# A graph layer on one core: six edges in a partition instead of eight, a written order with the MLP in pieces, and the check of dst at the end

## The chip, the cores and the metric

The kernel runs on one core of a Trainium2 chip. The metric is the device time of one launch in microseconds, taken as the median over runs.

## The reference

One layer of a graph network over 12,500 nodes and 412,500 edges, in fp32. `dst` (the second row of `edge_index`) is sorted.

```
h   = maximum(layernorm(x), 0)                        # x: 12500 x 128
agg = segment_sum(edge_attr_48, dst, 12500)           # edge_attr_48: 412500 x 48
z   = concatenate([h, agg, u], axis=1)                # u: 64 numbers, the same for every node
out = x + relu(z @ W1 + b1) @ W2 + b2                 # W1: 240 x 256, W2: 256 x 128
```

## The kernel before

**Edges.** The sum over edges is done as matmuls. A chunk is 1,024 consecutive edges, T = 8 in each of 128 partitions; a group is CG = 4 chunks, 4,096 edges, and there are 101 groups. Because `dst` is sorted, the edges of a chunk fall into a window of W = 48 consecutive nodes. VectorE compares each edge's node number, relative to its window's start (`rel`), with 0 to 47 (L194): that makes a one-hot tile `oh` of 32 x 48 columns per group. TensorE then multiplies, for each of the 32 sets of 128 edges, the edge attributes (weights, 128 x 48) with the one-hot (moving, 128 x 48) into one PSUM bank (L201). Even sets go to PSUM partitions 0 to 47, odd ones to 64 to 111, that is to the two halves of the array's columns. An fp32 matmul appears in the trace as two weight loads and two matmul instructions, so a group has 64 of each. VectorE adds the bank into `aggT` at a node that it reads from a register (`add`, L214). Edge tiles have 8 buffers and are loaded on SyncE's queue (L174).

**Nodes.** A block is 512 nodes (25 blocks, the first has 212). For each, `mlp` (L382 to L414) normalizes x on ScalarE (L390), transposes it on TensorE (L392), copies it to `hT` (L395), and for each half `a` of the hidden layer multiplies `hT` (L399) and `aggT` (L400) with weights of 128 columns, applies relu on ScalarE (L402), multiplies with `w2` (L407), adds `xb` (x + b2, made on GpSimd at L386) and stores. `normalize` (L364 to L380) does the statistics of up to four blocks at once: 16 pairs of L372 and L373.

**Order.** The program is written as groups 0 to 5, then the check of `dst`, then groups 6 to 100 with a whole `mlp` between groups when a block's edges are done. The framework's planner moves instructions by its own cost estimates: in the trace, 20 matmuls of L201 stand between the second and the third matmul instruction of L407. The check (L267 to L280) tests that all edges fall into their windows; a branch (L284) behind it holds a slow general pass. For these inputs all do, and the branch is not taken.

**Names used below.** `dst` becomes `rel` by `read_dst` (four pieces, with transposes at L237 and copies at L238). `load_x` (L353) loads x for up to four blocks into one of two buffers.

## Time and profile before

| what | us |
|---|---|
| median of 3 runs | 422.22 |
| lowest and highest | 418.25, 425.51 |
| the profiled execution | 418.65 |
| its span, first to last instruction | 416.9 |
| mean granted TensorE clock | 0.957 of full speed |
| DMA traffic | 95.20 MB |

The profile is of one execution. PE is the matmul part of TensorE and PEld its weight loads, which overlap. DVE is VectorE, ACT ScalarE, POOL GpSimd, SP SyncE. A matmul's recorded duration holds its latency; the pace is read from the starts of successive instructions. "[0.43 <-ACT hT L395]" behind a row means 0.43 us of idle time on that engine, ended by that instruction.

### The profile page before, as it was taken

The numbers are of one execution on the slowest core, as the hardware profiler recorded it, in microseconds if no ns is written. First come the engines' busy times: TensorE is split into PE (matmuls) and PEld (weight loads), VectorE is DVE, ScalarE is ACT, GpSimd is POOL, SyncE is SP. The second block draws the span as 40 slices with busy tenths as digits, with TensorE's granted clock in tenths as the row PEclk, the third lists the DMA queues.
The fourth block names the chain that finished last, engine by engine and source line by source line (L and its number), as shares of the span: only waits on it lengthen the run. The fifth ranks groups of instructions, "written<-read, shape, count | busy, mean of one in ns | idle before, by whom it ended". The sixth has DMA issues, their size and how long they took to land.

```text
span 416.9 us, 15948 instructions
## 1 busy us (share of the span) xinstructions
PE 342.9 (82%) x7193; PEld 270.0 (65%) x7194; DVE 283.7 (68%) x472; ACT 106.4 (26%) x193; POOL 81.0 (19%) x41
## 2 busy tenths in 40 slices
PE   0487569998699989898986997995979998888985
PEld 0377555785477677577565777774768776757853
DVE  7898598764965696786377788467675668629510
ACT  1140027312213303331230330330321332131231
POOL 9300021120221120222022022112022112203200
PEclk9995689999999999999899999999889999989999
DMA  5997693559847978877596697696583898654000
GB/s 163 323 370 264 207 346 126 188 197 308 286 141 239 323 255 304 281 248 233 179 322 217 225 316 233 192 342 219 198 302 109 257 325 270 194 198 156 29 13 39
DMA packets 61720, 95.20 MB, mean 228 GB/s; under 512 B 2760, under 2 KB 54996, under 8 KB 61649
## 3 DMA queue, kind: packets, MB, share of 16 engines
q1 hardware_dynamic: 57287, 87.26, 62.4%
q10 hardware_dynamic: 4362, 6.89, 4.7%
q8 instruction: 57, 0.93, 0.9%
q14 instruction: 14, 0.11, 0.1%
HBM read 87.74 MB, written 6.40 MB: 226 GB/s over the span
## 4 chain that ended last, share of the span: by engine, by line
PE 40%; issue 17%; DMA 10%; DVE 10%; POOL 5%; ACT 3%; DVEq 1%; ACTq 0%; POOLq 0%
PE ps L201 17%; DMA xt<-in_x_dram 10%; PE po L407 8%; PE ph L399 7%; PE ph L400 6%; POOL xb L386 5%; DVE oh L194 4%; DVE st L372 3%; ACT hT L395 3%; PE pt L392 2%; DVE mv L373 1%; DVE ot L409 1%; DVE aggT L214 1%; DVEq L207 1%; ACT hid L402 0%
## 5 line engine op out<-in xcount | busy, mean ns | idle before, releaser
L201 PE MATMUL ps<-oh,e 128*48 128x48 f32 x6448 | 175.8, 214 | 39.4 <-issue 17.7
L201 PEld LDWEIGHTS ps<-oh,e 128*48 128x48 f32 x6448 | 163.2, 130 | 53.8 <-DVE oh L194 21.9
L194 DVE TENSOR_TENSOR oh<-iota,rel 128x1536 f32<-128x1536 f32 (+1 forms) x101 | 194.0, 1936 | 2.3 <-ACT rel L238 1.3
L386 POOL TENSOR_TENSOR xb<-xt,b_sb 128x512 f32<-128x512 f32 (+1 forms) x25 | 67.7, 2709 | 313.6 <-DVE ot L409 273.6
L395 ACT COPY hT<-pt 128x512 f32<-128x512 f32 (+1 forms) x25 | 26.9, 1076 | 186.3 <-PE pt L392 186.3
L399 PE MATMUL ph<-hT,w1h 128*128 128x512 f32 (+1 forms) x100 | 56.4, 647 | 8.0 <-ACT hT L395 7.9
L214 DVE TENSOR_TENSOR aggT<-aggT,ps 112x141 f32 (+1 forms) x101 | 29.6, 293 | 47.8 <-PE ph L400 44.0
L407 PEld LDWEIGHTS po<-w,hid 128*128 128x128 f32 (+1 forms) x400 | 49.9, 189 | 16.5 <-issue 10.4
L407 PE MATMUL po<-w,hid 128*128 128x128 f32 (+1 forms) x400 | 55.4, 281 | 1.2 <-ACT hid L402 1.1
L409 DVE TENSOR_TENSOR ot<-po,xb 128x512 f32<-128x512 f32 (+1 forms) x25 | 17.2, 688 | 51.3 <-PE po L407 49.0
L400 PE MATMUL ph<-aggT,w1a 112*128 112x512 f32 (+1 forms) x100 | 52.0, 602 | 0.0
L402 ACT ACTIVATE hid<-ph,bias 128x512 f32<-128x512 f32 (+1 forms) x50 | 33.6, 676 | 47.5 <-PE ph L400 47.5
L390 ACT ACTIVATE xn<-xt,sh,sc 128x128 f32<-128x128 f32 (+1 forms) x100 | 40.7, 484 | 3.7 <-DVE sh L378 3.7
L372 DVE BATCH_NORM_STATS2 st<-xt 128x6 f32<-128x128 f32 (+1 forms) x100 | 25.1, 262 | 22.0 <-DMA xt<-in_x_dram 22.0
L400 PEld LDWEIGHTS ph<-aggT,w1a 112*128 112x128 f32 x100 | 20.3, 203 | 24.6 <-issue 24.0
L399 PEld LDWEIGHTS ph<-hT,w1h 128*128 128x128 f32 x100 | 18.3, 204 | 23.0 <-ACT hT L395 10.3
L392 PE MATMUL pt<-ident,xn 128*128 128x128 f32 (+1 forms) x100 | 18.1, 296 | 1.6 <-ACT xn L390 1.2
L373 DVE BATCH_NORM_AGGREGATE mv<-st 128x2 f32<-128x6 f32 (+1 forms) x100 | 15.6, 162 | 0.0
L246 PE MATMUL pb<-one,brow 1*128 1x1 f32 (+1 forms) x8 | 2.0, 312 | 14.6 <-DVE brow L141 13.8
L392 PEld LDWEIGHTS pt<-ident,xn 128*128 128x128 f32 (+1 forms) x100 | 11.1, 144 | 3.8 <-POOL xb L386 1.3
L376 ACT ACTIVATE sc<-mv,eps 128x16 f32<-128x16 f32 (+1 forms) x7 | 2.1, 305 | 42.0 <-DVE mv L373 42.0
L238 ACT COPY rel<-ptd 128x512 f32<-128x512 f32 (+1 forms) x8 | 6.7, 910 | 20.7 <-DMA w1a<-in_L_gnn_W_dram 13.4
(46 smaller groups left out, 59.9 us busy)
## 6 DMA issues: line engine op xcount, KB each, us to landing
e<-in_edge_attr_dram SPq DMA_DIRECT2D x100, 768.0 KB, 7.5
xt<-in_x_dram ACTq DMA_DIRECT2D x6, 1024.0 KB
out_dram<-ot SPq DMA_DIRECT2D x24, 256.0 KB, 5.3
di<-in_dst_dram SPq DMA_DIRECT2D x3, 512.0 KB, 11.1
e<-in_edge_attr_dram SPq DMA_DIRECT2D x1, 384.0 KB, 6.5
e<-in_edge_attr_dram SPq DMA_DIRECT2D x1, 159.0 KB
w1h<-in_L_gnn_W_dram ACTq DMA_DIRECT2D x1, 128.0 KB
w<-in_L_gnn_W_dram ACTq DMA_DIRECT2D x1, 128.0 KB, 4.2
```

The costliest lines, as they stand in the source:

```text
L194: nc.vector.tensor_tensor(oh[:, :n * T], iota[:, None, :W].to_broadcast([P, n * T, W]), r[:, :, None].to_broadcast([P, n * T, W]), OP.is_e ...
L201: nc.tensor.matmul(ps[h:h + DE, STEP * k:STEP * k + W], e[:, k, t * DE:(t + 1) * DE], oh[:, k * T + t, :], start=(k == 0 and t < 2), stop= ...
L214: nc.vector.tensor_tensor(aggT[:K2, ds(at, wg)], aggT[:K2, ds(at, wg)], ps[:K2, :wg], OP.add)
L372: nc.vector.bn_stats(st[:m, i * R + r, :], xs[j][:m, r, :])
L386: nc.gpsimd.tensor_tensor(xb[:m], xs[j][:m], b2_sb[:m, None, :].to_broadcast([m, R, D]), OP.add)
L390: nc.scalar.activation(xn[:m, r], xs[j][:m, r], AF.Relu, bias=shift[j][:m, r:r + 1], scale=scale[j][:m, r:r + 1])
L392: nc.tensor.transpose(pt[:, r, :m], xn[:m, r], ident[:m, :m])
L395: nc.scalar.copy(hT[:, :n].rearrange("d (p r) -> d r p", r=R), pt[:, :, :m])
L399: nc.tensor.matmul(ph[:, :n], w1h[:, a * P:(a + 1) * P], hT[:, :n], start=True, stop=False)
L400: nc.tensor.matmul(ph[:, :n], w1a[:K2, a * P:(a + 1) * P], aggT[:K2, SL + a0:SL + a0 + n], start=False, stop=True)
L402: nc.scalar.activation(hid[:, a, :, :m], ph[:, :n].rearrange("h (p r) -> h r p", r=R), AF.Relu, bias=bias[:, a:a + 1])
L407: nc.tensor.matmul(po[:m, r], hid[:, a, r, :m], w2[:, a], start=(a == 0), stop=(a == NH - 1))
```

## The change

- A chunk is 768 edges (T = 6), a group is 6 chunks, 4,608 edges: 90 groups. The window has W = 36 nodes and is placed from the node of the group's middle edge. A group has 36 sets of 128 edges, so 72 weight loads and 72 matmul instructions; a one-hot tile has 36 x 36 columns.
- The order is written out (`manual_schedule`). In turn g: `contract(g)` on TensorE, the one-hot of g+1, the load of group g+7 (7 edge buffers), `add(g-1)`, the store of a finished block, up to three steps of statistics, and at most two pieces of the MLP (`hidden(j, 0)`, `hidden(j, 1)`, `transpose(j+1)`, `output(j)`).
- In `hidden` and `output`, every matmul with 128 weight columns becomes two with 64 columns, to the two halves of the array's columns.
- `xb` moves from GpSimd to VectorE. L373 goes; a few operations per four blocks take its place. x has three buffers.
- At the start, the first three groups get their window numbers by a load of their own (`di0`, rows of 24 bytes, and `lo0`), `dst` is read in five pieces between groups, and `aggT` is zeroed by GpSimd and ScalarE.
- The check of `dst` is summed on ScalarE (`check_dst`), decided near the end, and the branch stands behind all stores; in it is a second pass over everything.

The core of the diff (the second pass, the bodies of the check and the constants of the start are left out):

```diff
-    T = 8
+    T = 6
     CE = P * T
-    CG = 4
+    CG = 6
     GE = CG * CE
-    STEP = N * CE // E
-    SL = 8
-    W = 48
-    WG = STEP * (CG - 1) + W
+    SL = 6
+    W = 36
+    OFF = [round(N * CE / E * (k - CG / 2)) - SL for k in range(CG)]
+    PAD = -OFF[0]
+    WG = OFF[-1] - OFF[0] + W
...
-    NB = -(-NCH // P)
+    GB = P // CG
+    CB = GB * CG
+    NB = -(-NG // GB)
+    FIRST = 3
...
+    XBUFS = 3
+    PF = 7
+    LAG = 2
+    GSTEP = N * GE / E
+    LEAST = int(-OFF[0] - SL - 64)
+    NC = N + PAD + P
...
+    supers += [rest[:1]] + [rest[i:i + XB] for i in range(1, len(rest), XB)]
+    super_of = {j: s for s, js in enumerate(supers) for j in js}
+
+
+    ready = [min(NG - 1, int(-(-(a + R * m + PAD + 1 - LEAST) // GSTEP)) - 1) for a, m in blocks]
+
+    ctx.enter_context(tc.manual_schedule())
...
+    def load_group(g):
+        if g < NG:
+            edges[g] = ep.tile([P, CG, T * DE], F32, name="e")
+            load_edges(edges[g], g * CG, chunks[g])
+
...
+        middle = dst[:FIRST * GE].rearrange("(a g e) -> a g e", a=1, e=GE)[:, :, GE // 2]
+        nc.sync.dma_start(lo0, middle.to_broadcast([P, FIRST]))
+        nc.sync.dma_start(di0, dst[:FIRST * GE].rearrange("(c p t) -> p c t", p=P, t=T))
+        load_group(0)
+        nc.sync.dma_start(first[:, :nf], dst[:nf * GE].rearrange("(a g e) -> a g e", a=1, e=GE)[:, :, GE // 2])
...
+        load_group(1)
+        dis = {0: load_dst(0)}
+        load_group(2)
...
+    cut = NC * 5 // 8
+    for c in range(0, cut, 1024):
+        nc.gpsimd.memset(aggT[:, c:min(c + 1024, cut)], 0.0)
...
+    load_x(0)
+    acc = []
+    for i in range(3):
+        ps = psum.tile([P, 512], F32, name=f"ps{i}")
+        nc.scalar.copy(ps, zero.to_broadcast([P, 512]))
+        acc.append(ps)
+    load_x(1)
+    nc.scalar.copy(aggT[:, cut:], zero.to_broadcast([P, NC - cut]))
+    warm = const.tile([P, 1], F32)
...
+    def onehot(g):
+        if g < NG:
+            n = chunks[g]
+            oh = ohp.tile([P, CG * T, W], F32, name="oh")
+            rel, c = (rel0, g * CG) if g < FIRST else (rels[g // GB], g % GB * CG)
+            r = rel[:, c:c + n, :].rearrange("p c t -> p (c t)")
+            nc.vector.tensor_tensor(oh[:, :n * T], iota[:, None, :].to_broadcast([P, n * T, W]),
+                                    r[:, :, None].to_broadcast([P, n * T, W]), OP.is_equal)
+            hots[g] = oh
+
+    def contract(g):
+        n, e, oh, ps = chunks[g], edges.pop(g), hots.pop(g), acc[g % len(acc)]
+        for k in range(n):
+            o = OFF[k] - OFF[0]
+            for t in range(T):
+                h = HI * (t % 2)
+                nc.tensor.matmul(
+                    ps[h:h + DE, o:o + W], e[:, k, t * DE:(t + 1) * DE], oh[:, k * T + t, :],
+                    start=(k == 0 and t < 2), stop=(k == n - 1 and t >= T - 2), skip_group_check=True)
+
+    def add(g):
+        wg = OFF[chunks[g] - 1] - OFF[0] + W
+        _, at = nc.values_load_multi_w_load_instructions(
+            lo_i[0:1, g:g + 1], engines=[DVE], min_val=0, max_val=N - 1,
+            skip_runtime_bounds_check_because="clamped to 0..N-1 on the chip")
+        to = aggT[:K2, ds(at[0], wg)]
+        nc.vector.tensor_tensor(to, to, acc[g % len(acc)][:K2, :wg], OP.add)
...
+    def shift_dst(b, di):
+
+        rows = rows_in[b]
+        pb = pst.tile([P, 1], F32, name="pt")
+        nc.tensor.matmul(pb[:rows], brow.rearrange("a g k -> a (g k)")[:, b * CB:b * CB + rows], one,
+                         start=True, stop=True)
+        nc.vector.tensor_copy(base[:rows, b:b + 1], pb[:rows])
+        df = dp.tile([P, CE], F32, name="df")
+        nc.vector.tensor_tensor(df[:rows], di[:rows], base[:rows, b:b + 1].to_broadcast([rows, CE]), OP.subtract)
+        return df
...
+    def spread(b, df):
+
+        rows = rows_in[b]
+        dv = df.rearrange("c (p t) -> c t p", t=T)
+        rels[b] = dp.tile([P, CB, T], F32, name="rel", bufs=2)
+        for t0 in range(0, T, 3):
+            pt = pst.tile([P, 3, P], F32, name="pt")
+            for t in range(3):
+                nc.tensor.transpose(pt[:, t, :rows], dv[:rows, t0 + t, :], ident[:rows, :rows])
+            nc.scalar.copy(rels[b][:, :rows, t0:t0 + 3].rearrange("p c t -> p t c"), pt[:, :, :rows])
+
+    def check_dst(b, df):
+
+        rows = rows_in[b]
+        for s, sign in ((0, -1.0), (1, 1.0)):
+            far = dp.tile([P, CE], F32, name="far")
+            nc.scalar.activation(far[:rows], df[:rows], AF.Relu, bias=bounds[:rows, s:s + 1], scale=sign,
+                                 accum_out=span[:rows, b, s:s + 1])
+
...
+        def variance():
+
+            me, qe, mo, qo = [st[:m, :q, i] for i in (1, 2, 4, 5)]
...
+            nc.scalar.activation(sc[:m, :q], va[:m, :q], AF.Sqrt, bias=eps[:m], scale=1.0 / D)
+
+        def finish():
+            nc.vector.reciprocal(sc[:m, :q], sc[:m, :q])
+            nc.vector.scalar_tensor_tensor(sh[:m, :q], su[:m, :q], -0.5, sc[:m, :q], OP.mult, OP.mult)
...
+                stats.append((s, lambda i=i, j=j, r=r: nc.vector.bn_stats(st[:m, i * R + r, :], xs[j][:m, r, :])))
+        stats.append((s, variance))
+        stats.append((s, finish))
...
+    def transpose(j):
+        m = blocks[j][1]
+        pt = pst.tile([P, R, P], F32, name="pt")
+        xn = xns.pop(j)
+        for r in range(R):
             nc.tensor.transpose(pt[:, r, :m], xn[:m, r], ident[:m, :m])
 
-        hT = mp.tile([P, BN], F32, name="hT")
-        nc.scalar.copy(hT[:, :n].rearrange("d (p r) -> d r p", r=R), pt[:, :, :m])
-        hid = mp.tile([P, NH, R, P], F32, name="hid")
-        for a in range(NH):
-            ph = psh.tile([P, BN], F32, name="ph")
-            nc.tensor.matmul(ph[:, :n], w1h[:, a * P:(a + 1) * P], hT[:, :n], start=True, stop=False)
-            nc.tensor.matmul(ph[:, :n], w1a[:K2, a * P:(a + 1) * P], aggT[:K2, SL + a0:SL + a0 + n],
-                             start=False, stop=True)
-            nc.scalar.activation(hid[:, a, :, :m], ph[:, :n].rearrange("h (p r) -> h r p", r=R),
-                                 AF.Relu, bias=bias[:, a:a + 1])
+        hT = mp.tile([P, P, R], F32, name="hT")
+        nc.scalar.copy(hT[:, :m], pt[:, :, :m].rearrange("d r p -> d p r"))
+        hTs[j] = hT.rearrange("d p r -> d (p r)")
+
+    def hidden(j, a):
+        a0, m = blocks[j]
+        n = R * m
+        if a == 0:
+            hids[j] = mp.tile([P, NH, R, P], F32, name="hid")
+            xb = mp.tile([P, R, D], F32, name="xb")
+            nc.vector.tensor_tensor(xb[:m], xs[j][:m], b2_sb[:m, None, :].to_broadcast([m, R, D]), OP.add)
+            xbs[j] = xb
+        ph = psh.tile([P, BN], F32, name="ph")
+        for c in (0, HI):
+            nc.tensor.matmul(ph[c:c + HI, :n], w1h[:, a * P + c:a * P + c + HI], hTs[j][:, :n],
+                             start=True, stop=False, skip_group_check=True)
+        for c in (0, HI):
+            nc.tensor.matmul(ph[c:c + HI, :n], w1a[:K2, a * P + c:a * P + c + HI], aggT[:K2, PAD + a0:PAD + a0 + n],
+                             start=False, stop=True, skip_group_check=True)
+        nc.scalar.activation(hids[j][:, a, :, :m], ph[:, :n].rearrange("h (p r) -> h r p", r=R),
+                             AF.Relu, bias=bias[:, a:a + 1])
+
+    def output(j):
+        m = blocks[j][1]
         po = pso.tile([P, R, D], F32, name="po")
         for r in range(R):
             for a in range(NH):
-                nc.tensor.matmul(po[:m, r], hid[:, a, r, :m], w2[:, a], start=(a == 0), stop=(a == NH - 1))
+                for c in range(0, m, HI):
+                    k = min(m, c + HI)
+                    nc.tensor.matmul(po[c:k, r], hids[j][:, a, r, c:k], w2[:, a], start=(a == 0), stop=(a == NH - 1),
+                                     skip_group_check=True)
+        pos[j] = po
+
+    def store(j):
+        a0, m = blocks[j]
         ot = mp.tile([P, R, D], F32, name="ot")
-        nc.vector.tensor_tensor(ot[:m], po[:m], xb[:m], OP.add)
+        nc.vector.tensor_tensor(ot[:m], pos.pop(j)[:m], xbs.pop(j)[:m], OP.add)
         k = m - m % 16
...
+    pieces = []
+    for j in range(len(blocks)):
+        at = ready[j] + LAG
+        if j == 0:
+            pieces.append((2, lambda j=j: transpose(j)))
+        pieces.append((at, lambda j=j: hidden(j, 0)))
+        pieces.append((at + 1, lambda j=j: hidden(j, 1)))
+        if j + 1 < len(blocks):
+            pieces.append((at + 2, lambda j=j: transpose(j + 1)))
+        pieces.append((at + 2, lambda j=j: output(j)))
...
+    def pop_piece():
+        nonlocal freed
+        pieces.pop(0)[1]()
+        if hTs:
+            prepare(max(hTs) + 1)
+        if freed < len(supers) and xbs and max(xbs) == supers[freed][-1]:
+            load_x(freed + XBUFS)
+            freed += 1
...
+    for g in range(NG + LAG):
+        if g < NG:
+            contract(g)
+            if g == 1:
+                spread(0, dfs[0])
+            onehot(g + 1)
+            load_group(g + PF)
+            b, i = divmod(g, GB)
+            if b + 1 < NB:
+                if i == GB - 14:
+                    dis[b + 1] = load_dst(b + 1)
+                elif i == GB - 9:
+                    dfs[b + 1] = shift_dst(b + 1, dis[b + 1])
+                elif i == GB - 7:
+                    spread(b + 1, dfs[b + 1])
+                elif i == GB - 5:
+                    check_dst(b + 1, dfs[b + 1])
+            if g == 0:
+                dfs[0] = shift_dst(0, dis[0])
+            elif g == 2:
+                first_bias()
+            elif g == 3:
+                check_dst(0, dfs[0])
+            elif g == NG - 6:
+                decide()
+        if 0 <= g - 1 < NG:
+            add(g - 1)
+        for j in late:
+            store(j)
+        for _ in range(3):
+            if stats:
+                stats.pop(0)[1]()
+        if g == 1:
+            prepare(0)
+        n = 0
+        while pieces and pieces[0][0] <= g and n < 2:
+            pop_piece()
+            n += 1
+        late = list(pos)
+    while pieces:
+        pop_piece()
...
+    isbad = nc.values_load(bad[0:1, 0:1], min_val=0, max_val=1,
+                           skip_runtime_bounds_check_because="clamped to 0..1 on the chip")
+    with tc.If(isbad >= 1):
```

## Rows read from the trace of the kernel before

**Rows 1.** The page's first part: busy time of each engine, share of the span, instructions.

```profile
span 416.9 us, 15948 instructions
PE 342.9 (82%) x7193; PEld 270.0 (65%) x7194; DVE 283.7 (68%) x472; ACT 106.4 (26%) x193; POOL 81.0 (19%) x41
```

**Rows 2.** Timeline of one block: start us, us, engine, line, operation, [idle before <-releaser].

```profile
323.54 1.10 ACT L395 COPY hT<-pt 128x512 f32<-128x512 f32 x1 [7.46 <-PE pt L392]
...
326.52 1.02 PE L399 MATMUL ph<-hT,w1h 128*128 128x512 f32 x2
...
327.38 1.02 PE L400 MATMUL ph<-aggT,w1a 112*128 112x512 f32 x2
...
328.55 0.53 PEld L201 LDWEIGHTS ps<-oh,e 128*48 128x48 f32 x20
...
329.18 1.64 PEld L407 LDWEIGHTS po<-w,hid 128*128 128x128 f32 x14
...
330.94 4.84 PEld L201 LDWEIGHTS ps<-oh,e 128*48 128x48 f32 x210
...
335.83 0.42 PEld L392 LDWEIGHTS pt<-ident,xn 128*128 128x128 f32 x4
...
336.48 0.70 PEld L201 LDWEIGHTS ps<-oh,e 128*48 128x48 f32 x26 [0.22 <-DVE oh L194]
...
336.59 1.10 ACT L395 COPY hT<-pt 128x512 f32<-128x512 f32 x1 [7.46 <-PE pt L392]
```

**Rows 3.** Weight loads of lines L201 and L407: duration in ns, min/median/max.

```profile
L201 PEld LDWEIGHTS ps<-oh,e x6448: 119/125/198, 23.2 to 404.4; 128*48 128x48 f32 x196
...
L407 PEld LDWEIGHTS po<-w,hid x400: 123/192/192, 63.5 to 412.4; 128*128 128x128 f32 x128, 128*53 128x53 f32 x6
```

**Rows 4.** Timeline from 93 to 111 us: x arrives, and what follows.

```profile
93.77 1.63 ACT L390 ACTIVATE xn<-xt,sh,sc 128x128 f32<-128x128 f32 x4
...
102.03 0.49 DVE L372 BATCH_NORM_STATS2 st<-xt 128x6 f32<-128x128 f32 x2 [5.71 <-DMA xt<-in_x_dram]
...
109.26 1.64 PE L201 MATMUL ps<-oh,e 128*48 128x48 f32 x64 [2.64 <-DVE oh L194]
...
110.83 0.66 PE L392 MATMUL pt<-ident,xn 128*128 128x128 f32 x4
```

**Rows 5.** The hT copies on ScalarE, one per block: first full, around that arrival, last.

```profile
67.78 1.11 ACT L395 COPY hT<-pt 128x512 f32<-128x512 f32 x1 [0.30 <-PE pt L392]
...
92.88 1.11 ACT L395 COPY hT<-pt 128x512 f32<-128x512 f32 x1 [7.40 <-PE pt L392]
111.53 1.11 ACT L395 COPY hT<-pt 128x512 f32<-128x512 f32 x1 [11.62 <-PE pt L392]
...
405.36 1.05 ACT L395 COPY hT<-pt 128x512 f32<-128x512 f32 x1 [2.78 <-PE pt L392]
```

**Rows 6.** Timeline of the start, up to the first instruction behind the branch L284.

```profile
23.22 4.44 PE L201 MATMUL ps<-oh,e 128*48 128x48 f32 x128 [0.67 <-DVE oh L194]
...
28.34 2.07 ACT L238 COPY rel<-ptd 128x512 f32<-128x512 f32 x2 [4.66 <-PE ptd L237]
...
45.71 0.52 PEld L344 LDWEIGHTS po<-u,w1u 64*128 64x128 f32 x4 [2.75 <-PEq L284]
```

**Rows 7.** Groups by form: line, shapes, count, busy us, mean ns, idle before.

```profile
L194 DVE TENSOR_TENSOR oh<-iota,rel 128x1536 f32<-128x1536 f32 x100 | 191.8, 1933 | 2.3 <-ACT rel L238 1.3 <-PE ps L201 0.8
```

**Rows 8.** DMA over the whole span, all queues.

```profile
DMA packets 61720, 95.20 MB, mean 228 GB/s; under 512 B 2760, under 2 KB 54996, under 8 KB 61649
```

**Rows 9.** DMA queues from 91 to 102 us: packets, MB, share of 16 engines' time.

```profile
q1 hardware_dynamic: 2040, 3.08, 77.4%
q10 hardware_dynamic: 528, 1.05, 26.3%
```

**Rows 10.** The same for ScalarE's queue in the first 20 us.

```profile
q10 hardware_dynamic: 1056, 0.44, 8.5%
```

**Rows 11.** Timeline: the last compute instruction of the span.

```profile
412.87 0.69 DVE L409 TENSOR_TENSOR ot<-po,xb 128x512 f32<-128x512 f32 x1 [7.45 <-PE po L407]
```

More of the change, by code (lines that the diff above doesn't have):

```diff
@@ L101 @@
     span = const.tile([P, NB, 2], F32)
+    base = const.tile([P, NB], F32)
     bad = const.tile([1, 1], I32)
-    first = const.tile([1, NG], I32)
-    with nc.allow_non_contiguous_dma(reason="a hundred numbers, once"):
-        nf = E // GE
-        nc.sync.dma_start(first[:, :nf], dst[:nf * GE].rearrange("(a g e) -> a g e", a=1, e=GE)[:, :, 0])
-        if nf < NG:
-            nc.sync.dma_start(first[:, nf:NG], dst[None, nf * GE:nf * GE + 1])
-    one = const.tile([1, 1], F32)
-    nc.gpsimd.memset(one, 1.0)
@@ L166 @@
-    ep = ctx.enter_context(tc.tile_pool(name="edges", bufs=8))
-    ohp = ctx.enter_context(tc.tile_pool(name="oh", bufs=3))
     def load_edges(e, c0, n):
@@ L345, with load_dst @@
-    nc.vector.tensor_tensor(bias, pb, b1_sb, OP.add)
-    xs, scale, shift = {}, {}, {}
+    chunks = [min(CG, NCH - g * CG) for g in range(NG)]
+    rows_in = [min(CB, NCH - b * CB) for b in range(NB)]
+    edges, hots, rels = {}, {}, {}
+    def load_group(g):
+        if g < NG:
+            edges[g] = ep.tile([P, CG, T * DE], F32, name="e")
+            load_edges(edges[g], g * CG, chunks[g])
+    def load_dst(b):
+        rows = rows_in[b]
+        full = min(CB, NFULL - b * CB)
+        di = dp.tile([P, CE], I32, name="di", bufs=2)
+        nc.sync.dma_start(di[:full], dst[b * CB * CE:(b * CB + full) * CE].rearrange("(c e) -> c e", e=CE))
+        if full < rows:
+            for q in range(0, CE, TAIL):
+                n = min(TAIL, CE - q)
+                nc.sync.dma_start(di[full:rows, q:q + n], dst[None, E - n:E])
+        return di
@@ L362, in load_x @@
             xs[j] = xt[:, i].rearrange("p (r d) -> p r d", d=D)
-    def normalize(s):
+    di0 = const.tile([P, FIRST * CG, T], I32)
+    lo0 = const.tile([P, FIRST], I32)
+    first = const.tile([1, NG], I32)
+    mids = [min(g * GE + GE // 2, E - 1) for g in range(NG)]
+    nf = min(sum(m == g * GE + GE // 2 for g, m in enumerate(mids)), E // GE)
+    w1h = const.tile([D, H], F32)
+    w1a = const.tile([P, H], F32)
+    w1u = const.tile([G, H], F32)
+    w2 = const.tile([P, NH, D], F32)
+    b1_sb = const.tile([P, NH], F32)
@@ new lines @@
+    zero = const.tile([P, 1], F32)
+    nc.gpsimd.memset(zero, 0.0)
+    iota = const.tile([P, W], F32)
+    nc.gpsimd.iota(iota, pattern=[[1, W]], base=0, channel_multiplier=0,
+                   allow_small_or_imprecise_dtypes=True)
+    offs = const.tile([P, CG], F32)
+    for k in range(CG):
+        nc.gpsimd.memset(offs[:, k:k + 1], float(OFF[k]))
+    most = const.tile([P, 1], F32)
+    nc.gpsimd.memset(most, float(N - 1))
+    one = const.tile([1, 1], F32)
+    nc.gpsimd.memset(one, 1.0)
@@ L365, in normalize, with first_bias, statistics @@
+    def first_bias():
+        pb = pst.tile([P, NH], F32, name="pt")
+        for a in range(NH):
+            nc.tensor.matmul(pb[:, a:a + 1], w1u[:, a * P:(a + 1) * P], u, start=True, stop=True)
+        nc.vector.tensor_tensor(bias, pb, b1_sb, OP.add)
+    stats = []
+    def statistics(s):
         js = supers[s]
@@ L434 @@
-    for w in waiting:
-        add(*w)
-    while nextm < len(blocks):
-        mlp(nextm)
-        nextm += 1
+    pieces = []
[8 more added lines that the diff above has]
+        pieces.append((at + 2, lambda j=j: output(j)))
@@ new lines, with prepare @@
+    begun = 0
+    prepared = 0
+    freed = 0
+    def prepare(upto):
+        nonlocal begun, prepared
+        while prepared <= min(upto, len(blocks) - 1):
+            s = super_of[prepared]
+            while begun <= min(s + 1, len(supers) - 1):
+                statistics(begun)
+                begun += 1
+            while stats and stats[0][0] <= s:
+                stats.pop(0)[1]()
+            normalize(prepared)
+            prepared += 1
+    def pop_piece():
[6 more added lines that the diff above has]
+            freed += 1
@@ new lines @@
+    first_nodes()
+    statistics(0)
+    begun = 1
+    dfs = {}
+    late = []
+    for g in range(NG + LAG):
[29 more added lines that the diff above has]
+            if stats:
+                stats.pop(0)[1]()
+        if g == 1:
[5 more added lines that the diff above has]
+        late = list(pos)
```

389 lines of the change are left out of this document (159 added, 230 removed).

## The prediction

> **What bounds the kernel now.** I read the page's busy times first. PE is busy for 342.9 of 416.9 us and DVE for 283.7 [rows 1]; both shares are means over stages, so the timeline of one block comes next. From hT copy to hT copy it takes 13.05 us [rows 2]. In it 256 edge matmuls run: 190 of them lie between 0.53 and 4.84 us, so one every 22.7 ns, 5.8 us in all. Two hidden matmul instructions take 0.86 us, so 0.43 each, and the eight 3.4 us. L407's fourteen weight loads take 1.64 us with a last one of 0.19, so one every 111.5 ns, and sixteen 1.8 us [rows 2]. That is 11.0 of 13.05 us. The rest is what lies between kinds of matmul. From the start of the 20 edge loads to L407 is 0.63 us, 0.18 more than their pace; from L407 to the edges 1.76 us, 0.20 more than its pace; from the 210 edge loads through the four transposes to the next edge 5.54 us, 0.77 more than the edges' pace [rows 2]. Then PE waits for the hT copy. So an undisturbed block is TensorE's.
>
> The mean block is longer: 24 blocks lie between 67.78 and 405.36 us, 14.07 us each, and one took 18.65 [rows 5]. What happened there: x arrived late, DVE began 32 statistics instructions at 102.03, the one-hot came late, and PE stood still for 2.64 us [rows 4]. The last part is the start: edges begin at 23.22 us, and the branch holds PE for another 2.75 us [rows 6].
>
> **The change, part by part.** I price the new order as TensorE's sum, since the written order is meant to leave PE nothing to wait for; whether it does is a rival below. MLP terms are for 24.4 blocks of 512 nodes (12,500 / 512).
>
> *Edges.* 412,500 edges in sets of 128 stay 3,228 sets and 6,456 instructions. The moving side falls from 48 to 36 columns, the weight side stays at 48. From below: the pace follows the columns, 22.7 x 36/48 = 17.0 ns, 109.8 us. From above: it doesn't fall, 22.7 ns, 146.6 us. Weight loads speak for the upper part: 48 columns take 125 ns and 128 take 192 [rows 3], 0.84 ns a column, so 40 ns stream for 48 columns; two halves of the array share that, 20 ns an instruction. I take the middle of 20 and 22.7: 21.3 ns, **137.5 us**.
>
> [...]
>
> *Hidden layer.* Eight instructions of 128 weight columns become sixteen of 64, in the order two for one half of the array, two for the other. If both halves always ran together, time stays 8 x 0.43 = 3.44 us a block, 83.9 us. But if instructions start in the order written, the first of a piece runs alone (the second needs the same half), and so does the last: five steps of 0.43 instead of four, twice a block, 4.30 us, **104.9 us**. The trace has TensorE in order: four transposes whose input was done at 95.40 ran only at 110.83, behind an edge matmul that waited for its one-hot [rows 4]. So I take five steps.
>
> [...]
>
> *Output.* 32 instructions in pairs, one alone at each end, 17 steps of 111.5 ns, 1.90 us, **46.3 us**.
>
> *Transposes* keep both changes of kind, 0.77 us a block [rows 2]: **18.8 us**. The other two changes, 0.18 and 0.20, go: hidden, output and edges now all use column halves. The hT copy is covered by a whole group of edges; with that cover gone it costs 1.1 us a block.
>
> *dst.* Five pieces, each six transposes at 0.65/4 us and one wait for a ScalarE copy, since the buffer is single: half of 2.07 us [rows 6]. 2.0 us each, **10.1 us**.
>
> Sum for TensorE: 137.5 + 104.9 + 46.3 + 18.8 + 10.1 = 317.6 us.
>
> *Start.* The first seven groups carry little MLP, and their data set their time. Until group 6 is there: 7 x 0.885 MB of edges, 1.42 MB of x, 0.39 of dst, 0.49 of weights, 8.5 MB. At full load the queues moved 4.13 MB in 11 us, 375 GB/s [rows 9]: 22.7 us. Before them go 2,688 tiny packets (di0 and lo0). The nearest price is 8.5% of 16 x 20 us over 1,056 packets, 25.8 ns [rows 10]; over 16 engines 4.3 us. At the 66.8 ns of a full-size packet (77.4% of 176 us over 2,040 [rows 9]) it is 11.2, at nothing 0. Then a one-hot and a group of matmuls, 1.6 + 1.5. So group 6 ends at 30 us, with 15.6 us of TensorE's sum done: **14.4 us** idle, 10 to 21.
>
> *End.* Waits for add and relu, about one ScalarE pass as hT's, 1.1 us [rows 2]; add, store and end 4.0 us [rows 11]; the branch 2.75 us [rows 6]: **7.9 us**. The second pass is not run: all edges fall into the new windows too, by two nodes or more for these inputs.
>
> *VectorE* must stay hidden. The one-hot of 1,296 columns is 1.933 x 1296/1536 = 1.63 us [rows 7], 147 us in all instead of 194; xb adds 25 x 0.69 us [rows 11]; L373 goes. Some 240 us under a stretch of 310: hidden, by about 0.8 us a turn of 3.5. Without that cover each late one-hot is PE's.
>
> *DMA* must too. In one window a packet of 1,510 bytes took 66.8 ns and one of 1,989 (26.3% of 176 us over 528) 87.7 ns [rows 9]: 0.044 ns a byte each, so I price by bytes. 95.2 MB [rows 8], less the first 8.5, in 300 us is 289 GB/s against 375. SP's queue holds load g+7 behind group g, then a store behind VectorE; six groups of about 3.5 us are loaded ahead, so a late store is covered. ScalarE (106.4 us [rows 1]) takes the check and the zeroing in its idle time.
>
> **Total.** 317.6 + 14.4 + 7.9 = 339.9 us of span. Before, the execution had 418.65 for a span of 416.9, and the median of runs is 422.22, 0.9% more: (339.9 + 1.75) x 1.0085 = **345 us**.
>
> **The rivals.**
>
> *The edges follow the columns* (17.0 ns): 28 us less, 317. [...] If the pace doesn't fall at all: 354, inside the forecast.
>
> *The halves of the hidden layer leave no gap:* 21 us less, 324. Against it: the order [rows 4]. Both together: 296.
>
> *A new wait takes the place of the old.* In the written order each piece has its fixed turn; if once a block PE waits for a ScalarE copy or a late one-hot as before, at 1.1 us [rows 2], 27 us more: 372. Single buffers for transposes speak for it, the covers above against it.
>
> *DMA becomes the bound.* If a packet costs 66.8 ns whatever its size, 68,750 edge packets take 287 us, the other 16 MB 43 us; with 4.3 us before and about 18 behind the last edges that is 352 of span, 357. Against it: the two sizes in rows 9.
>
> *Slower than before: the column halves of the MLP don't run side by side.* Then hidden takes 16 x 0.43 us a block, 63 us more, and output 32 steps, 41 more: 450. It decides against the change once over 80% of the overlap is lost (430.7 is 2% above 422.2). Against it: 48 columns stream for 40 ns, yet edge instructions start every 22.7 [rows 2, 3], so the halves do overlap there.
>
> **How the numbers follow.** Forecast 345 (332 to 358): 0.46. Edges by columns 0.17, no gap 0.12, both 0.06, a new wait 0.12, DMA by count 0.03, halves one after the other 0.04. The range 312 to 375 takes in all but "both" and "halves". About 2% is what a measurement here can tell from no change; faster by over 2%: 0.94, within 2%: 0.02, slower: 0.04, from the last rival and its partial forms.
>
> **What would show it.** Right: edge matmuls every 20 to 22.7 ns; ten steps of 0.43 us for a block's hidden layer; changes of kind only around transposes; first edges at 10 to 15 us and group 6 done near 30; PE without idle rows over 0.5 us between 35 and 325 us; DVE busy near 240 us. Wrong: PE rows ended by DVE oh or by DMA e in most turns; a pace of 17 ns; hidden pieces of 1.7 us; or hidden pieces of 3.4 us.

## The result and the profile after

The changed kernel takes **370.5 us** (median of 4 runs, 364.3 to 374.9), against 420.2 for the kernel before in the same session: 0.881 of it, 95% interval 0.850 to 0.911. A second session of 6 runs gave 370.3 us (367.4 to 372.9) and 0.885, 0.878 to 0.892. The forecast was 345, the range 312 to 375.

The profiled execution, at 374.9 us the slowest of the four, has a span of 373.0 us where the prediction summed 339.9. Busy times and two DMA queues, from the page of after, beside [rows 1, 8]:

```profile
PE 319.1 (86%) x7785; PEld 252.2 (68%) x7786; DVE 219.9 (59%) x412; ACT 114.6 (31%) x221; POOL 9.0 (2%) x32
...
q1 hardware_dynamic: 78290, 87.81, 74.9%
...
q8 instruction: 63, 1.03, 1.2%
```

TensorE's waits in after (cause: us in total, times, longest):

```profile
PE ps L277 <- issue: 22.4, 18, 2.2
PE ps L277 <- DMA e<-in_edge_attr_dram: 12.6, 2, 11.4
PE pt L320 <- ACT rel L321: 4.1, 5, 0.9
PE ph L421 <- DVE aggT L287: 3.2, 4, 1.7
PE ps L277 <- DVE oh L267: 1.8, 1, 1.8
```

The kernel before had these, among others:

```profile
PE ps L201 <- issue: 17.7, 13, 3.0
PE ps L201 <- DVE oh L194: 17.3, 14, 2.6
...
PE ph L399 <- ACT hT L395: 7.9, 16, 1.2
```

The waits for the one-hot and for the hT copy [rows 2, 4] are nearly gone. The largest row is one that names no releaser: 22.4 us of "issue" (23.2 with two small rows at L433 and L402). And this is the timeline of TensorE over a block, to be laid beside [rows 2] (start, duration, what, idle time before it):

```profile
217.45 1.81 PE L277 MATMUL ps<-oh,e 128*48 128x36 f32 x71
219.05 0.62 PE L418 MATMUL ph<-hT,w1h 128*64 128x512 f32 x1
219.09 0.21 PE L277 MATMUL ps<-oh,e 128*48 128x36 f32 x1
219.13 1.05 PE L418 MATMUL ph<-hT,w1h 128*64 128x512 f32 x3
219.94 1.10 PE L421 MATMUL ph<-aggT,w1a 112*64 112x512 f32 x4
220.80 1.85 PE L277 MATMUL ps<-oh,e 128*48 128x36 f32 x72
222.59 0.66 PE L402 MATMUL pt<-ident,xn 128*128 128x128 f32 x4
223.17 1.97 PE L433 MATMUL po<-w,hid 128*64 128x128 f32 x32
224.97 1.24 PE L277 MATMUL ps<-oh,e 128*48 128x36 f32 x48
227.70 0.73 PE L277 MATMUL ps<-oh,e 128*48 128x36 f32 x24 [1.49 <-issue]
```

A group of edges takes 1.60 us (72 instructions, 22.4 ns each), a hidden piece 1.75 us (219.05 to 220.80), transposes and output 2.38. For two groups TensorE does nothing but this, and then it stands still for 1.49 us in the middle of a group, after 48 of its 72 matmuls.

Summed over the execution, from start to start of successive matmuls with the waits taken out (the step into a transpose counts with the transposes):

| term | forecast, us | measured, us |
|---|---|---|
| edges | 137.5 | 154.9 |
| hidden | 104.9 | 88.6 |
| output | 46.3 | 46.4 |
| transposes | 18.8 | 18.8 |
| dst | 10.1, of it 5.2 waits | 9.6 and 0.6 for the bias, without waits |
| TensorE | 317.6 | 318.9 |
| idle, waits that end before 46 us | 14.4 | 19.5 |
| idle after that | none but dst's (above) | 28.2, of it issue 20.0 |
| end, after the last matmul | 7.9 | 6.3 |
| span | 339.9 | 373.0 |

TensorE's sum came out right by luck: two of its terms are wrong by 17 us in opposite directions. The miss of 33 us is idle time. A second profiled execution (the control below, 370.8 us) has nearly the same sums, 318.2 us of TensorE's work and 44.3 of its idle time.

### The profile page after: what moved, and what is told of

The parts are those of the page before. It is cut to its first block, busy times and chain, and to the rows that moved or that the text cites. A ratio compares the mean times of both kernels' runs of the same rounds, so it can differ in the third digit from the quotient of the medians.

```text
span 373.0 us, 16970 instructions
## 1 busy us (share of the span) xinstructions
PE 319.1 (86%) x7785; PEld 252.2 (68%) x7786; DVE 219.9 (59%) x412; ACT 114.6 (31%) x221; POOL 9.0 (2%) x32
## 3 DMA queue, kind: packets, MB, share of 16 engines
q8 instruction: 63, 1.03, 1.2%
## 4 chain that ended last, share of the span: by engine, by line
PE 80%; issue 7%; DMA 4%; SPq 4%; DVE 2%; ACT 1%; DVEq 0%
PE ps L277 38%; PE po L433 13%; PE ph L421 12%; PE ph L418 11%; PE pt L402 4%; DMA e<-in_edge_attr_dram 3%; DMA w1a<-in_L_gnn_W_dram 2%; SPq L131 2%; PE pt L320 1%; ACT rel L321 1%; SPq L203 1%; SPq L157 1%; SPq L256 1%; DVE oh L267 0%; DVE ot L440 0%
## 5 line engine op out<-in xcount | busy, mean ns | idle before, releaser
L277 PE MATMUL ps<-oh,e 128*48 128x36 f32 x6456 | 169.8, 215 | 36.8 <-issue 22.4
L267 DVE TENSOR_TENSOR oh<-iota,rel 128x1296 f32<-128x1296 f32 x90 | 134.4, 1494 | 0.0
L287 DVE TENSOR_TENSOR aggT<-aggT,ps 112x153 f32 x90 | 28.0, 311 | 58.7 <-PE ph L421 53.4
L421 PE MATMUL ph<-aggT,w1a 112*64 112x512 f32 (+1 forms) x200 | 53.9, 599 | 3.6 <-DVE aggT L287 3.2
L418 PE MATMUL ph<-hT,w1h 128*64 128x512 f32 (+1 forms) x200 | 55.3, 611 | 0.0
L433 PE MATMUL po<-w,hid 128*64 128x128 f32 (+1 forms) x784 | 51.1, 281 | 1.1 <-ACT hid L423 0.6
L433 PEld LDWEIGHTS po<-w,hid 128*64 128x64 f32 (+1 forms) x784 | 44.8, 140 | 6.3 <-issue 5.1
L421 PEld LDWEIGHTS ph<-aggT,w1a 112*64 112x64 f32 x200 | 16.4, 140 | 31.6 <-issue 21.2
L405 ACT COPY hT<-pt 128x512 f32<-128x512 f32 (+1 forms) x25 | 14.4, 576 | 40.5 <-PE pt L402 40.4
L402 PE MATMUL pt<-ident,xn 128*128 128x128 f32 (+1 forms) x100 | 16.7, 288 | 2.0 <-ACT rel L321 0.9
L414 DVE TENSOR_TENSOR xb<-xt,b_sb 128x512 f32<-128x512 f32 (+1 forms) x25 | 17.0, 679 | 0.0
L402 PEld LDWEIGHTS pt<-ident,xn 128*128 128x128 f32 (+1 forms) x100 | 10.5, 142 | 4.3 <-issue 1.7
L418 PEld LDWEIGHTS ph<-hT,w1h 128*64 128x64 f32 x200 | 11.7, 141 | 2.6 <-issue 2.3
```

The source lines that it names most:

```text
L267: nc.vector.tensor_tensor(oh[:, :n * T], iota[:, None, :].to_broadcast([P, n * T, W]), r[:, :, None].to_broadcast([P, n * T, W]), OP.is_equal)
L277: nc.tensor.matmul(ps[h:h + DE, o:o + W], e[:, k, t * DE:(t + 1) * DE], oh[:, k * T + t, :], start=(k == 0 and t < 2), stop=(k == n - 1 an ...
L287: nc.vector.tensor_tensor(to, to, acc[g % len(acc)][:K2, :wg], OP.add)
L402: nc.tensor.transpose(pt[:, r, :m], xn[:m, r], ident[:m, :m])
L414: nc.vector.tensor_tensor(xb[:m], xs[j][:m], b2_sb[:m, None, :].to_broadcast([m, R, D]), OP.add)
L418: nc.tensor.matmul(ph[c:c + HI, :n], w1h[:, a * P + c:a * P + c + HI], hTs[j][:, :n], start=True, stop=False, skip_group_check=True)
```

## Why TensorE stands still: experiments on the instruction blocks

The next rows are the timeline between two of the issue rows:

```profile
39.94 1.63 PE L277 MATMUL ps<-oh,e 128*48 128x36 f32 x63 [1.86 <-issue]
41.50 0.66 PE L402 MATMUL pt<-ident,xn 128*128 128x128 f32 x4
42.09 1.84 PE L433 MATMUL po<-w,hid 128*53 128x128 f32 x15
43.67 0.28 PE L277 MATMUL ps<-oh,e 128*48 128x36 f32 x2
43.77 0.27 PE L433 MATMUL po<-w,hid 128*53 128x128 f32 x1
43.88 1.14 PE L277 MATMUL ps<-oh,e 128*48 128x36 f32 x42
46.36 0.33 PE L277 MATMUL ps<-oh,e 128*48 128x36 f32 x6 [1.34 <-issue]
```

Between them run 63 + 4 + 15 + 2 + 1 + 42 = 127 matmuls and as many weight loads, about 256 instructions. Counted so, with the few semaphore instructions that the trace lists among them, all 19 rows over 0.3 us that name no releaser lie at places that leave 193 or 194 when divided by 256. In the kernel before, ten of eleven leave 216 or 217. And queue 8 moved 63 packets of 16 KB, one for about 250 of TensorE's 15,571 instructions. So, as I read these counts, TensorE's program comes in blocks of 256 instructions, each by DMA, and TensorE waits when a block is late, 22.4 us in the rows above. In after a packet begins a median of 2.0 us after TensorE has passed the place before (up to 6.5) and takes 1.1 us; at every issue row work resumes 1.3 to 1.6 us after the packet's end.

**Control.** The changed kernel again, beside the next two and the one without column halves.

> The changed kernel itself, beside the variants of the same call, so that they are compared on one chip. Its profiled execution had a span of 373.0 us with 22.4 us of TensorE idle rows that end with issue, and its times ran from 364 to 375 us. Both theories expect 364 to 375 us again and 18 to 25 us of such rows; fewer than 12 us would mean that they are an accident of one execution and explain nothing.

370.3 us. Its issue rows, 19.3 us in all, as expected:

```profile
PE ps L277 <- issue: 17.1, 14, 3.2
...
PE pt L320 <- issue: 1.3, 1, 1.3
...
PE po L433 <- issue: 0.9, 2, 0.6
```

**No edge loads after the start.**

```diff
-            edges[g] = ep.tile([P, CG, T * DE], F32, name="e")
-            load_edges(edges[g], g * CG, chunks[g])
+            edges[g] = e_buf[g % PF]
+            if g < PF:
+                load_edges(edges[g], g * CG, chunks[g])
```

(Not shown: the seven edge buffers become seven tiles with names of their own, e_a to e_g, here and wherever loads come in pieces below.)

> Left out: from group 7 on no edges are loaded; TensorE contracts the first seven groups' tiles again and again, so the sums are of other edges. All instructions of TensorE, VectorE and ScalarE stay. Theory (late instruction blocks): the idle rows that end with issue lie 256 TensorE instructions or a multiple of it apart, and the 16 KB packets of the instruction queue come late because edge loads fill the DMA engines. Then with the DMA nearly empty after the start these rows fall from 22.4 us to under 6 (what is left lies before 45 us), the wait for edges (12.6 us) stays, being the start's, and the time falls by 15 to 25 us to 343 to 355. Rival (the block change itself costs, whatever the DMA does): the rows stay at 18 to 25 us and the time within 364 to 375. Second rival (TensorE waited for loads in a form that the rows do not name): rows and time fall too, but the instruction packets would be no earlier against TensorE's work.

343.6 us (341.9 to 344.9). Queue 1 and TensorE's waits, from the page and the waits of this kernel:

```profile
q1 hardware_dynamic: 13574, 14.80, 13.6%
...
q8 instruction: 63, 1.03, 1.2%
```

```profile
PE ps L279 <- DMA e_a<-in_edge_attr_dram: 11.5, 1, 11.5
...
PE ps L279 <- issue: 0.7, 2, 0.5
```

The same 63 blocks, the same 15,571 matmuls and weight loads, and the issue rows fall to 0.7 us; a packet now begins about 0.5 us after its place (median). The first theory holds, both rivals fall: the blocks are late because edges fill the DMA. The time falls by 26.7 us: 18.6 are the rows. In the two profiled executions TensorE's own sum falls too, by 9.3 us: 10 us of its work start in stretches granted 0.50 instead of 21, which is worth 5; the other 4 were not traced.

**Loads in single chunks.**

```diff
-            load_edges(edges[g], g * CG, chunks[g])
+            if g < PF:
+                load_edges(edges[g], g * CG, chunks[g])
+            else:
+                for k in range(chunks[g]):
+                    load_edges(edges[g][:, k:k + 1], g * CG + k, 1)
```

> Nothing left out: from group 7 on each chunk of 144 KB is loaded by itself as soon as TensorE has read that chunk's buffer, 540 loads instead of 90, so that less stands queued in the DMA engines at any time. Theory (an instruction packet waits behind queued edge packets): idle rows that end with issue fall from 22.4 us to 5 to 12, time to 350 to 362 us. Rival (the volume alone makes the packets late, not the queue): rows at 18 to 25 us, time 364 to 375. Second rival (SyncE's issues, 540 at 0.37 us or 200 us in all, and the waits among them make edges late): TensorE rows ended by DMA e grow past 20 us and the time is above 375.

391.8 us: the second rival's time, though not by the rows that it named; those ended by edges are 17.3 us, 11.6 of them at the start. Issue rows are down to 1.5 us, but other waits took their place. TensorE's, and VectorE's timeline where the worst of them ends:

```profile
PE ph L426 <- DVE aggT L292: 19.7, 4, 7.4
```

```profile
156.18 0.96 DVE L314 TENSOR_TENSOR df<-di,base 126x768 f32<-126x768 int32 x1 [7.87 <-DMA di<-in_dst_dram]
```

SyncE fell behind: at 149.8 us it loaded group 35 while TensorE was at 34, where after runs about six ahead. Its loads use eight semaphores in turn, and in this trace nearly every load begins only when the load before it on the same semaphore has landed, a median of 1 us earlier (13 us in after). That this holds SyncE back is a reading; no run has another number of them. So the load of dst, which stands in its queue, came late, VectorE stood before L314 and its adds with it. Because TensorE waited there, the missing issue rows prove nothing here.

**Loads in thirds of a group.**

```diff
-            load_edges(edges[g], g * CG, chunks[g])
+            step = chunks[g] if g < PF else 2
+            for k in range(0, chunks[g], step):
+                n = min(step, chunks[g] - k)
+                load_edges(edges[g][:, k:k + n], g * CG + k, n)
```

> Nothing left out: from group 7 on the load of a group is issued in three pieces of two chunks, 288 KB each, as TensorE reads the chunks before them. With single chunks (540 loads) the issue rows had gone, 1.5 us, but SyncE ran only one to three groups ahead of TensorE instead of seven and dst came up to 7.9 us late. Theory (the packet of instructions waits behind queued edge packets; eight loads of 288 KB under way are enough for the pace): issue rows 3 to 10 us, no row ended by edges or dst over 2 us after the start, 352 to 364 us. Rival (the issue rows went only because TensorE stood elsewhere): 14 to 22 us of issue rows, 364 to 373 us. Second rival (loads fall behind here too): TensorE rows ended by DVE aggT and DMA e above 15 us, over 375 us.

360.9 us (358.5 to 364.2), ratio 0.857, 0.852 to 0.861. Time as the theory said; no late dst; the issue rows are just above its 3 to 10 us, instead of 19.3:

```profile
PE ps L281 <- issue: 11.1, 14, 2.9
```

Nearly the whole difference lies in these rows, but a packet's median delay is no shorter (1.9 us, as in the control). From 25 to 45 us the DMA's load is lower, 0.92 of its engines and 298 GB/s against 1.08 and 358, but few of the rows lie there, and with eight edges (below) pieces lower the rows while the load stays at 1.05. How the pieces help in detail stays open.

## The parts of the change

**Without the column halves.**

```diff
-        for c in (0, HI):
-            nc.tensor.matmul(ph[c:c + HI, :n], w1h[:, a * P + c:a * P + c + HI], hTs[j][:, :n],
-                             start=True, stop=False, skip_group_check=True)
+        nc.tensor.matmul(ph[:, :n], w1h[:, a * P:(a + 1) * P], hTs[j][:, :n],
+                         start=True, stop=False, skip_group_check=True)
```

(and the same for L421 and L433)

> Nothing left out: the column halves of hidden and output are undone, 128 weight columns each as before the change, everything else of the change stays. Theory (two halves in the order two and two take four steps of 0.43 us, so the halves save only changes of kind): a hidden piece takes 1.72 us and 0.38 more for its changes before and after, twice a block, 0.76 x 24.4 = 18.5 us more; output 16 x 111.5 ns = 1.78 instead of 1.90, 3 us less; 2,340 TensorE instructions fewer are 9 blocks of 256 fewer, 3 us less: 12 us slower than the changed kernel, 377 to 388. Rival (a change of kind costs nothing between pieces that stand between groups): 358 to 370. Second rival (the halves run in fewer steps than their count and are the main gain of the change): over 390.

373.1 us, ratio 0.892, 0.887 to 0.897: 0.7% above the changed kernel (0.878 to 0.892), hardly clear of noise, between the theory and the first rival. The trace shows two effects. TensorE's sum grew by 11 us, from the hidden layer:

```profile
202.20 1.81 PE L277 MATMUL ps<-oh,e 128*48 128x36 f32 x72
203.94 1.12 PE L417 MATMUL ph<-hT,w1h 128*128 128x512 f32 x2
204.91 1.02 PE L419 MATMUL ph<-aggT,w1a 112*128 112x512 f32 x2
205.86 1.93 PE L277 MATMUL ps<-oh,e 128*48 128x36 f32 x72
```

A group and a piece take 3.66 us here (202.20 to 205.86) and 3.35 in after (217.45 to 220.80): changes of kind do cost 0.31 a piece. Transposes and output cost the same 2.4 us in both. What gave most of that back: 1,168 instructions fewer (not the 2,340 that I had expected), 58 blocks instead of 63, and issue rows of 11.7 us instead of 19.3.

**Without the six edges.**

```diff
-    T = 6
+    T = 8
...
-    CG = 6
+    CG = 4
...
-    SL = 6
-    W = 36
+    SL = 8
+    W = 48
```

(and the transposes of dst in fours instead of threes)

> Nothing left out: eight edges in a partition, four chunks in a group and windows of 48 columns again (as before the change), in the new order and with the column halves. Theory (for TensorE six edges brought 0.3 ns an instruction, for the DMA they cost 13% a byte): edges at 22.7 ns, 2 us more; edge packets of 1,536 bytes again, so a packet of instructions waits less and idle rows that end with issue fall from 17 to 22 us to 8 to 14; one-hots 101 x 1.93 = 195 us of VectorE instead of 134, still covered: 362 to 370 us, against 370.3 for the changed kernel in the last call. Rival (the room that the narrow windows gave VectorE was needed): TensorE rows ended by DVE oh or DVE aggT grow by over 10 us, 375 to 395. Second rival (neither matters): 368 to 373 with 17 to 22 us of issue rows.

363.1 us (361.4 to 367.3), ratio 0.861, 0.857 to 0.865, against the control's 0.878 to 0.892. The time is the theory's; six edges in a partition, with the windows and groups that go with them, made the change 7 us slower. But the mechanism holds only in small part: issue rows are 17.0 us, not 8 to 14, and all of TensorE's waits are 46.4 us against the control's 44.3. What fell is TensorE's own sum, 311.6 us against 318.2: 8.8 us of its work start in stretches granted 0.50, against 20.8, worth 6. Over the runs, too, the clock is 0.985 against 0.973. Nor was a byte 13% dearer: the edge queue took 0.0509 ns a byte and engine in after and 0.0490 here, 4%. VectorE's room was not needed: 260.7 us busy, and 2.7 us of waits for one-hots beside the first.

**Rows of 768 bytes,** everything else as in the last one.

```diff
-            nc.sync.dma_start(
-                e[:, :f], edge_attr[c0 * CE:(c0 + f) * CE].rearrange("(c p t) d -> p c (t d)", p=P, t=T))
+            rows = edge_attr[c0 * CE:(c0 + f) * CE].rearrange("(c p t) d -> p c (t d)", p=P, t=T)
+            for s in (slice(0, T * DE // 2), slice(T * DE // 2, T * DE)):
+                nc.sync.dma_start(e[:, :f, s], rows[:, :, s])
```

> Nothing left out: eight edges in a partition as run before (363.1 us), but every load of edges in two of 768 bytes a row instead of one of 1,536, so that packets are half as long and twice as many, and nothing else differs. Queue 1 was busy for 0.0477 ns a byte and engine in the kernel before, 0.0509 with rows of 1,152 bytes, 0.0490 with rows of 1,536 in the new order. Theory (six edges in a partition lost 7 us because shorter packets cost more a byte and keep instruction packets waiting): 0.053 to 0.060 ns a byte, issue rows from 17 us to over 25, 370 to 385 us. Rival (a packet's length costs nothing here, and the 7 us are of the low clock and the groups' size): 0.048 to 0.050, 361 to 366 us.

371.3 us (368.7 to 374.3): 8.2 us more, the theory's time, at 0.0525 ns a byte and engine, just under its band. But its issue rows, 16.2 us, are not the place. From 25 to 45 us, where the DMA is full, three kernels moved (rows of 1,152, 1,536 and 768 bytes in this order):

```profile
DMA packets 5935, 7.16 MB, mean 358 GB/s; under 512 B 153, under 2 KB 5419, under 8 KB 5931
```

```profile
DMA packets 4810, 7.39 MB, mean 369 GB/s; under 512 B 172, under 2 KB 4294, under 8 KB 4806
```

```profile
DMA packets 8045, 6.69 MB, mean 335 GB/s; under 512 B 269, under 2 KB 7530, under 8 KB 8042
```

So shorter packets do cost rate here. The edit also halves each load, but that isn't the cause: with loads of 393 KB in whole rows (eight edges in pieces, below) the same window moves

```profile
DMA packets 4792, 7.21 MB, mean 361 GB/s; under 512 B 268, under 2 KB 4276, under 8 KB 4788
```

At 50 us this kernel has 639 matmul instructions behind it, the one with whole rows 703. Over the whole execution TensorE waits no longer, 43.9 us against 46.4; its own sum is longer, 321.0 against 311.6, and 23.1 us of it start in stretches granted 0.50, against 8.8, which is 7 of these 9 us. So the time went to the low clock. That late data in the start lead to it is a reading; no run holds the clock alone.

**What sets the pace of the edges.**

```diff
-                    ps[h:h + DE, o:o + W], e[:, k, t * DE:(t + 1) * DE], oh[:, k * T + t, :],
+                dw, mw = ((DE, W), (DE // 2, W), (DE, W // 2))[g % 3]
+                    ps[h:h + dw, o:o + mw], e[:, k, t * DE:t * DE + dw], oh[:, k * T + t, :mw],
```

> Left out: in groups 1, 4, 7, ... only 24 of the 48 feature columns are loaded as weights, in groups 2, 5, 8, ... only 18 of the 36 window columns are moved; groups 0, 3, 6, ... are whole. Asked is the pace of an edge instruction in each kind, 22.4 ns in whole groups. The forecast's reading (40 ns of weight stream for 48 columns, two halves share it): 24 weight columns 12 to 18 ns, 18 moving columns 22.4. Rival (a floor for the start of an instruction pair, whatever the columns): 22 to 23 ns in all three. [...]

```profile
202.80 3.40 PE L278 MATMUL ps<-oh,e 128*48 128x18 f32 x144
206.02 1.62 PE L419 MATMUL ph<-hT,w1h 128*64 128x512 f32 x3
...
208.87 1.36 PE L278 MATMUL ps<-oh,e 128*24 128x36 f32 x72
210.15 1.08 PE L419 MATMUL ph<-hT,w1h 128*64 128x512 f32 x4
```

The 144 instructions up to 206.02 are a group with 18 moving columns and a whole one behind it, 22.4 ns each. Group by group (mean from start to start, median over the groups at full clock) 18 moving columns take 22.0 ns, whole instructions 22.1, and 24 weight columns 16.3. The forecast's reading holds in its direction: the weights set the pace, and the moving columns, at these sizes, none of it. But half the columns take off 5.8 ns and not half the pace; what the rest is stays open.

**TensorE at work before the first edges.**

```diff
+    hot = const.tile([P, P], F32)
+    nc.vector.memset(hot, 0.0)
+    pw = pst.tile([P, P], F32, name="pt")
+    for i in range(34):
+        nc.tensor.matmul(pw, hot, hot, start=True, stop=True)
     load_x(0)
```

> Nothing left out: 34 matmuls of 128 zero columns are added before the first edges, in the 11.4 us in which TensorE has nothing to do. In the changed kernel the first 72 edge instructions took 3.10 us, 43 ns each, against 1.61 us later. Theory (TensorE starts at its low clock since it stood still): the first 72 take 1.6 us and the start shortens by what edges and dst that land allow, 1 to 4 us: 366 to 369 us against 370.3. Rival (the start goes by what lands, and a faster clock only turns into waiting): 369 to 372 us with longer rows ended by DMA e and ACT rel. Second rival (added instructions push more blocks through the instruction queue in the busiest stretch): over 372.

370.8 us against 370.3: the rival's time. The first 72 edge instructions took 1.81 us instead of 3.10, then TensorE waited for edges, dst and copies, though not longer than before (copies 4.1 us in both), and the granted clock fell to 0.50 at 20.6 us for 13.7 us: the groups at 21.22, 26.18 and 29.75 us took 3.10 us each.

## A faster version

Three kernels put the edits together: T = 8, CG = 4 and the loads in pieces in all three, windows of 46 and the output layer below in the last two.

```diff
-    SL = 6
-    W = 36
+    SL = 7
+    W = 46
...
-                for c in range(0, m, HI):
-                    k = min(m, c + HI)
-                    nc.tensor.matmul(po[c:k, r], hids[j][:, a, r, c:k], w2[:, a], start=(a == 0), stop=(a == NH - 1),
-                                     skip_group_check=True)
+                nc.tensor.matmul(po[:m, r], hids[j][:, a, r, :m], w2[:, a], start=(a == 0), stop=(a == NH - 1),
+                                 skip_group_check=True)
```

> Nothing left out: eight edges in a partition as run before (363.1 us), and the load of a group in two pieces of 393 KB from group 7 on; the output layer keeps its halves. Theory (queued edge packets make instruction packets late): issue rows fall from 17.0 us to 8 to 12 and the time to 353 to 358 us. Rival (pieces this large change nothing, a group's whole load is 786 KB): 361 to 365 us with 15 to 20 us of issue rows.

Eight edges, windows of 48 and loads of two chunks: 359.0 us (357.6 to 362.2), 0.854; issue rows 12.1 us. A miss by 1 us: beside eight edges alone (0.857 to 0.865) the pieces gave 4 us, within the noise (0.848 to 0.861), where they gave 9 beside six.

> Nothing left out: the changed kernel with eight edges in a partition, four chunks in a group and windows of 46 columns, a group's load in two pieces of 393 KB from group 7 on, and the output layer with all 128 columns again; hidden keeps its halves. Theory (each part works on the lateness of instruction packets or on TensorE's sum by itself): 363.1 us for eight edges, less 8 for the pieces (issue rows 19 to 11 us with six edges), less 2 to 3 for the output (53.0 us with its changes in halves against 50.8 in full columns, and three instruction blocks fewer): 350 to 356 us. Rival (eight edges and pieces relieve the same lateness, so the second gives nothing): 359 to 363 us.

With the output layer in full columns and windows of 46 besides: 358.8 us (354.3 to 359.4), 0.852. Issue rows 8.6 us, 60 blocks. Between the theory and the rival: about nothing over the last one.

> Nothing left out: the combined kernel with a load for each chunk, 196 KB, 400 loads instead of 200. Theory (what is queued counts, and 196 KB loads keep up where 144 KB loads did not): issue rows under 6 us and 347 to 354 us. Rival (as with 144 KB pieces of six edges, SyncE falls behind TensorE and dst comes late): TensorE rows ended by DVE aggT, DVE df or DMA e above 15 us, over 362 us.

The same with a load for each chunk: **355.1 us** (353.7 to 359.3), ratio 0.848, 0.841 to 0.856, the lowest median of all, 1 us above the theory's band; the interval overlaps those of the last two, so the gain over them isn't shown. Here loads of 196 KB keep up, mostly four to six and a half groups ahead, where those of 144 KB did not. TensorE's longest waits, beside those of after:

```profile
PE ps L281 <- DMA e_a<-in_edge_attr_dram: 10.8, 1, 10.8
PE ps L281 <- issue: 6.0, 6, 1.5
PE ph L425 <- DVE aggT L291: 5.6, 5, 2.3
```

## Why the prediction was right or wrong

**The direction and the size of the gain** were right, 50 us of the forecast 77, though the time lies above the forecast's 332 to 358. Between the profiled executions TensorE's idle time fell from 69.2 to 47.6 us and its own sum, taken in the same way, from 343.3 to 318.9. What carries the gain, by what is left, is the written order with what moved along with it: without the halves the gain is 48 us, without six edges it is larger. The order alone was not run, so this is not shown.

**Edges, 21.3 ns.** Mis-sized by 1.1 ns: 22.4, within the bounds [rows 2], 7 us. Of the other 10 us of this term some 6 are low clock (12.4 us of edges ran before 19.5 us, where no clock is recorded, and in stretches granted 0.50, at half pace); the rest lies behind waits and at beginnings of groups. 72 instructions take 1.61 us in mid-run but 3.10 in the first two groups and 2.77 at 34.36, granted clock 0.50 from 29.8 to 36.6. Before, too, the clock was 0.957; the sum had every row at 1.00.

**Hidden, five steps.** This step failed, 16 us the other way. A piece takes four steps of 0.43 us, 1.75 in all, near the 1.7 that the prediction named as a sign that it was wrong. In the timeline above an edge matmul of one half (219.09) starts after the first L418 of the other (219.05), though it stands ahead of it in the program. At 215.70 the second half's first L418 starts 0.08 us after the first's, and the first half's second 0.46 after. So in this trace the halves each follow their own order, and [rows 4], from which I took it for the whole engine, shows only that four transposes stood behind an edge matmul that waited 2.64 us for its one-hot. The rival "no gap" had the right mechanism.

**Output and transposes** were right to 0.1 us, and the changes of kind stand only around the transposes (18.8 us with them). For output that is luck: a block takes 1.80 us (223.17 to 224.97), sixteen steps and not the seventeen that its in-order reading gave; one block at the low clock (3.11 us) and the small first block make up the difference. **dst** was too low: its 10.1 us held 5.2 of waits for copies; measured are 9.6 us of work alone and 4.1 of such waits among the idle time.

**The start.** First edges at 11.39 us, within the 10 to 15 that the prediction named. Group 6 ended at 41.5 us instead of 30: not for its edges, which TensorE waited for only twice (12.6 us), but for the one-hot of group 4 (1.8 us), two late blocks (3.2), copies, and the low clock. The idle time of 19.5 us lies within the stated 10 to 21.

**DMA by bytes.** 0.0509 ns a byte over the span against 0.0477 before; I had taken 0.044 for all packet sizes from one window [rows 9]. That the DMA is not the bound was right, and incomplete: what it makes late is not edges but TensorE's own program, by 22.4 us of waits.

**VectorE** is busy for 219.9 us instead of 240: the one-hot takes 1.49 us, not 1.63. It stayed hidden but for 5.8 us of TensorE's waits.

**The idle time in mid-run** is the step that was missing. The sum left TensorE nothing to wait for after 46 us but dst; it waited for 28.2 us, 20.0 of them for blocks. The rival "a new wait takes the place" has nearly this price (27 us, 372), but named a ScalarE copy or a late one-hot. The wait isn't new either: the kernel before had 17.7 us of it in 13 rows, which the prediction did not price.

**The end**, 6.9 with its last wait instead of 7.9, was right.

## What to carry to other kernels

Sum the waits by releaser before pricing a change, and ask of rows without a releaser whether they lie a fixed count of instructions apart: here the count was 256, TensorE's own program was 63 packets and 1.03 MB of traffic, and with the DMA full of edges it came late, for 19.3 us of waits against 0.7 without those loads. Loads in pieces that still run ahead took off 9 us (six edges), and with five blocks fewer these waits fell from 19.3 to 11.7 us, which gave back most of the 11 us that full columns added to TensorE's sum. Price the clock too: a sum made at a granted clock of 1.00 leaves out what runs at 0.50, where a group of edges took 3.10 us (the run with matmuls before the first edges), against 1.81 at 1.00 (in after, at 24.90 us). In after the four stretches granted 0.50 before the last matmul, 17 us, each begin within 1.3 us of the end of a wait of 0.9 to 2.2 us. That the waits are the cause is a reading.

## What the runs showed of the hardware that I had not expected

- TensorE's 15,571 matmuls and weight loads came in 63 packets of 16 KB, one per 256 instructions by the places of the late ones; waits for these took 19.3 us of 369 with edges loading and 0.7 of 341 without.
- The two column halves of the array each kept their own order: eight instructions in two halves took 1.75 us, four steps of 0.43 and not five.
- From 25 to 45 us, with its engines full, the DMA moved 335, 358 and 369 GB/s with edge rows of 768, 1,152 and 1,536 bytes.
- With 128 x 48 weights 18 or 36 moving columns made no difference (22.0 and 22.1 ns); 24 weight columns brought 16.3.
